# Graph attention on one core: where the head outputs are divided, how one layer's are stored, and at which tiles a head pair's end is issued

## The chip, the cores and the metric

The kernel runs on one core of one Trainium2 chip. The metric is the device time of one execution in microseconds. Engines are named as in the profile: PE is TensorE's matmuls and PEld its weight loads, DVE is VectorE, ACT ScalarE, POOL GpSimd, SP the queue that issues most DMAs. A line such as L598 is a line of the kernel before, unless it is said to be one of the changed kernel.

## The reference

A graph of N = 2708 nodes with 512 features goes through four residual layers, each ended by a layer norm. Layers 0 and 1 are neighbour means with dense weights. Layers 2 and 3 are graph attentions:

```
Wh = h @ W[head]                       8 heads of 64 features
e  = leaky_relu(f1[n] + f2[m], 0.2), masked by the adjacency
head output = softmax(e) @ Wh          heads side by side: [N, 512]
layer 2:  x = layernorm(x + heads)
layer 3:  x1 = elu(heads); one more attention with one head of 512;
          elu, two dense layers; x = layernorm(x + that)
```

A softmax row divides by its sum. The kernel leaves the products with Wh undivided, computes the sums beside them, and divides the outputs.

## The kernel before

The nodes are cut into NT = 22 tiles of 128 rows. The mask lies transposed in SBUF for the whole run (maskT). After layers 0 and 1 the stages that matter here follow each other:

- project (L502, "p2" and "p3") makes Wh of one layer. For each tile, a source function delivers 512 features a row (plain L758 or summed L761), PE transposes them in four 128x128 steps (L120), ACT copies the result to xT (L122), and PE multiplies with the weights in 16 instructions (L529, 32 records a pair of tiles). DVE takes two columns out (dcol L534, b L536) and scales the product into R2 (L543); ACT makes exponentials of the columns (ecol L538, ucol L539, vcol L549, vrow L557). Loads are made one tile ahead, with three buffers for rows. In "p3", summed loads layer 2's head outputs from o_dram and the residual from x2_dram, adds them on DVE (L764), and normalises: bn_stats (L108), bn_aggr (L110), a small addition (L112), a power on POOL (L113), and the multiply on DVE (L114). It stores the row tile through POOL's queue (L766).
- heads_attention (L613, "a2" and "a3") is the long stage. The output nodes are cut into two blocks of 11 tiles (1408 and 1300 wide). For each block and each pair of heads (eight "runs"), a loop goes over 22 tiles j. For each j and head DVE makes the weights e (L598; four buffers, so two tiles j), ACT a comparison c in fp8 (L606; eleven buffers), and PE adds six products to po (L734). Every fourth j, PE adds the divisor products of the last four j to pd from c (L665, "burst").
- The end of a pair is a generator, finish (L668), of which one step is taken in each j of the next pair: the rest of the divisor products and a copy dT (L635); at j=2 the fold of dT into sums by three small matmuls (L643); at j=3, 5 and 7 the turns, transposes of oT in groups of four tiles (L686); behind the first of them the divisor itself by five small DVE operations (rc, L710 to L714); after each turn a DVE multiply that divides and moves the group from PSUM to SBUF (L696) and a store to o_dram (L702, L704). oT is a copy of po that ACT makes at the pair's end (L743).
- masks (L646) makes the part of the sums that needs only the mask, once a block, before the block's first pair is finished: 88 matmuls (L651), for the second block in steps of four j that follow the pair end.
- project "p4" has elu_first (L769) as its source: rows of o_dram, then ELU by four operations (L753 to L756), then the same transposes. last_attention and the dense layers follow. The tile lin (L896) holds their weights and hT; two 2 MB loads (L789, L790) fill it.

The order of TensorE's instructions inside heads_attention is the order in which the code issues them: pe() (L95) chains each to the one before. All other orders are a scheduler's, from program order and its own costs. [...]

Of the kernel before, what the change touches and what calls it, by code (L numbers as in the profile page):

```python
# [30 lines left out]
def kernel(  # L31
# [56 lines left out]
    z1_dram = dram.tile([N, D], F32, name="z1_dram")  # L88
    x2_dram = dram.tile([N, D], F32, name="x2_dram")
    x3_dram = dram.tile([N, D], F32, name="x3_dram")  # L90
    o_dram = [dram.tile([N, D], F32, name=f"o_dram{i}") for i in range(2)]

    behind = []

# [8 lines left out]
    def as_it_comes(ins):  # L103
        return ins

    def layer_norm(pool, y, n, dst):
        st = pool.tile([P, 6], F32, name="ln_st")
        nc.vector.bn_stats(st[:n], y)  # L108
        mv = pool.tile([P, 2], F32, name="ln_mv")
        nc.vector.bn_aggr(mv[:n], st[:n])  # L110
        rs = pool.tile([P, 1], F32, name="ln_rs")
        nc.vector.tensor_scalar(rs[:n], mv[:n, 1:2], EPS, None, op0=OP.add)  # L112
        nc.gpsimd.tensor_tensor(rs[:n], rs[:n], half[:n], OP.pow)  # L113
        nc.vector.tensor_scalar(dst, y, mv[:n, 0:1], rs[:n], op0=OP.subtract, op1=OP.mult)  # L114

    def transposed(pool, psum, src, n, name, order=as_it_comes):

# [368 lines left out]
    ecol = late.tile([P, NT, H], F32, name="ecol")  # L486
    for c in (ucol, ecol, vcol, bcol):
        nc.gpsimd.memset(c, 0.0)
    okc = const.tile([P, 4], F32, name="okc")
    nc.vector.tensor_scalar(rdeg, iso, 0.0, None, op0=OP.is_equal, op1=OP.add, accum_out=okc[:, 3:4])  # L490
    expected = float(P * NT * (3 * H + 1))
# [7 lines left out]
        nc.vector.tensor_sub(rest, rest, dst[:, :, :, 1])  # L499
        nc.vector.tensor_copy(dst[:, :, :, 2], rest)  # L500

    def project(name, source, layer, v_dram, cuts):  # L502


        w_src, w_view, _, heads = atts[layer]
# [9 lines left out]
        with ExitStack() as ph:  # L515
# [4 lines left out]
            width = max(z - a for a, z in cuts) * P  # L520
            xs = early(1, NT, lambda t: source(sm, t, rows(t)))
            xTs = early(0, NT, lambda t: transposed(ahead, ps_tr, xs(t), rows(t), "xT"))
            for t in range(NT):
                n = rows(t)
                xT = xTs(t)
# [84 lines left out]
    cuts = [-((-NT * i) // nb) for i in range(nb + 1)]  # L610
    blocks = list(zip(cuts[:-1], cuts[1:]))

    def heads_attention(name, att, dst):  # L613

        with ExitStack() as ph:
# [28 lines left out]
            def masks(b, p):  # L646

                c00 = att.blocks[b][0] * P
                for j in range(NT):
                    for g, c0, c1 in groups(b):  # L650
                        pe(nc.tensor.matmul(p[32 * g:32 * g + 3 * H, :c1 - c0], parts_m[:, j].rearrange("p h i -> p (h i)"),  # L651
                                            maskT[:, j, c00 + c0:c00 + c1], start=(j == 0), stop=(j == NT - 1)))
                    if j % 4 == 3:
                        yield
                dT = copied(p)
                yield
                ps = folded(dT, pick_m.rearrange("p g h -> p (g h)"))
                yield
                nc.vector.tensor_copy(sums_m[b].rearrange("p (g t) h -> p t g h", g=4), ps)

            def divisors(b, p, pair):
                for j, hs, cs in pair:
# [3 lines left out]
                                                start=(j == 0 and h == hs[0]), stop=(j == NT - 1 and h == hs[1])))  # L666

            def finish(b, h0, p, pair, oT):  # L668
                t0, t1 = att.blocks[b]
                nt = t1 - t0  # L670

                divisors(b, p, pair)
                dT = copied(p)
                yield
                yield
                sums = folded(dT, pick_c.rearrange("p g k q -> p (g k q)")).rearrange("p t g (k q) -> p t g k q", k=2)
                yield
                full = min(t1, FULL) - t0
                rc = sm.tile([P, 12, 2], F32, name="rc")
                by = lambda x_: x_.rearrange("p (g t) k -> p t g k", g=4)  # L680

                def turned(a0):
                    ps = ps_t.tile([P, 512], F32, name="ps_t").rearrange("p (t c) -> p t c", c=P)
                    for t in range(a0, min(a0 + 4, nt)):
                        n = rows(t0 + t)
                        pe(nc.tensor.transpose(ps[:n, t - a0, :], oT[:, a0 // 4, (t - a0) * P:(t - a0) * P + n], ident))  # L686
                    return ps

                def divided(a0, ps):
                    a1 = min(a0 + 4, nt)  # L690
                    o = sm.tile([P, 4, P], F32, name="o", bufs=3)
                    for n, a, z in [(P, a0, min(a1, full)), (rows(NT - 1), max(a0, full), a1)]:
                        if a >= z:
                            continue
                        m = z - a
                        nc.vector.tensor_mul(o[:n, a - a0:z - a0].rearrange("p t (k c) -> p t k c", k=2),  # L696
                                             ps[:n, a - a0:z - a0].rearrange("p t (k c) -> p t k c", k=2),
                                             rc[:n, a:z, :, None].to_broadcast([n, m, 2, HO]))
                        r0 = (t0 + a) * P
                        rows_ = dst[r0:r0 + (m - 1) * P + n, h0 * HO:(h0 + 2) * HO]  # L700
                        if n == P:
                            nc.sync.dma_start(rows_.rearrange("(t p) c -> p t c", p=P), o[:, a - a0:z - a0])  # L702
                        else:
                            nc.sync.dma_start(rows_, o[:n, a - a0])  # L704

                for a0 in range(0, nt, 4):
                    ps = turned(a0)
                    yield
                    if a0 == 0:
                        nc.vector.tensor_mul(by(rc), sums[:, :, :, :, 1], by(vcol[:, t0:t0 + 12, h0:h0 + 2]))  # L710
                        nc.vector.tensor_add(by(rc), by(rc), sums[:, :, :, :, 0])
                        nc.vector.tensor_add(rc, rc, sums_m[b][:, :, h0:h0 + 2])
                        nc.vector.tensor_scalar(rc, rc, 1e-30, None, op0=OP.max)
                        nc.vector.reciprocal(rc, rc)  # L714
                    divided(a0, ps)
                    yield

            sums_m = [sm.tile([P, 12, H], F32, name="sums_m") for b in range(len(att.blocks))]
            for _ in masks(0, pd[1]):
                pass  # L720
            todo = iter(())
            for r, (b, h0) in enumerate(runs):
                w = att.width(b)
                parts = [(c, min(c + 4 * P, w)) for c in range(0, w, 4 * P)]
                hs = (h0, h0 + 1)
                vs = [att.load(b, h) for h in hs]
                po = [ps_o.tile([P, 512], F32, name="po", tag="po") for _ in parts]
                pair = []
                for j in range(NT):
                    es = [att.weights(b, h, j, v) for h, v in zip(hs, vs)]  # L730
                    cs = [att.above(b, h, j, e) for h, e in zip(hs, es)]
                    for i, (c0, c1) in enumerate(parts):
                        for k, (h, e) in enumerate(zip(hs, es)):
                            pe(nc.tensor.matmul(po[i][HO * k:HO * k + HO, :c1 - c0], R2[:, j, h * HO:(h + 1) * HO],  # L734
                                                e[:, c0:c1], start=(j == 0), stop=(j == NT - 1)))
                    if len(pair) == 4:
                        divisors(b, pd[r % 2], pair)
                        pair = []
                    pair.append((j, hs, cs))
                    next(todo, None)  # L740
                oT = sm.tile([P, 3, 512], F32, name="oT", bufs=1)
                for i, (c0, c1) in enumerate(parts):
                    nc.scalar.copy(oT[:, i, :c1 - c0], po[i][:, :c1 - c0])  # L743
                todo = finish(b, h0, pd[r % 2], pair, oT)
                if h0 == H - 4 and b + 1 < len(att.blocks):
                    todo = chain(todo, masks(b + 1, pd[r % 2]))
            for _ in todo:
                pass

    def elu(pool, dst, src, n, w):  # L750

# [8 lines left out]

    def summed(sm, t, n):  # L761

        o, x2 = fetched(o_dram[0], t, n), fetched(x2_dram, t, n, late, "spare", 2)
        nc.vector.tensor_add(o, o, x2)  # L764
        layer_norm(late, o, n, o)
        nc.gpsimd.dma_start(x3_dram[t * P:t * P + n, :], o)  # L766
        return o

    def elu_first(sm, t, n):  # L769
        o = fetched(o_dram[1], t, n)  # L770
        elu(late, o, o, n, D)
        return o

    class Last:
# [111 lines left out]
            pass  # L886

    vd = [dram.tile([heads, N], F32, name=f"v_dram{i}") for i, heads in enumerate((H, H, 1))]
    for i, (source, dst) in enumerate(((plain, o_dram[0]), (summed, o_dram[1]))):
        with ExitStack() as ph:  # L890
            att = Weights(ph, f"a{2 + i}", blocks, vd[i])
            project(f"p{2 + i}", source, i, vd[i], blocks)
            heads_attention(f"a{2 + i}", att, dst)
    ph4 = fast.enter_context(ExitStack())
    att = Weights(ph4, "a4", quads, vd[2])
    lin = ph4.enter_context(tc.tile_pool(name="lin", bufs=1)).tile([P, KD * FF + KF * D + KD * 512], F32, name="lin")  # L896
    project("p4", elu_first, 2, vd[2], quads)


    bad = const.tile([1, 1], mybir.dt.int32, name="bad")  # L900
# [325 lines left out]
```

## Time and profile before

Three runs took 3123.17, 3125.3 and 3129.33 us (median 3125.3); the profiled one has a span of 3125.8 us at a granted clock of 0.996.

| Engine | busy us | share |
|---|---|---|
| PE | 3009.5 | 96% |
| DVE | 1988.8 | 64% |
| ACT | 1401.3 | 45% |
| POOL | 223.2 | 7% |

The shares are an average over stages with different limits, and matmuls are pipelined, so that a busy PE is not PE at its peak; what bounds a stage is read from the waits in it. By the trace the stages stand at: layers 0 and 1 until 925 us, projection 2 until 1025, head attention 2 until 1612, projection 3 until 1715, head attention 3 until 2308, projection 4 until 2404, and the last attention with the dense layers to the end. The copies of oT mark the ends of pairs: 1103, 1178, 1252, 1327, 1396, 1466, 1536 and 1606 us in head attention 2.

### The profile page before, as it was taken

The numbers are of one execution on the slowest core, as the hardware profiler recorded it, in microseconds if no ns is written. First come the engines' busy times: TensorE is split into PE (matmuls) and PEld (weight loads), VectorE is DVE, ScalarE is ACT, GpSimd is POOL, SyncE is SP. The second block draws the span as 40 slices with busy tenths as digits, with TensorE's granted clock in tenths as the row PEclk, the third lists the DMA queues.
The fourth block names the chain that finished last, engine by engine and source line by source line (L and its number), as shares of the span: only waits on it lengthen the run. The fifth ranks groups of instructions, "written<-read, shape, count | busy, mean of one in ns | idle before, by whom it ended". The sixth has DMA issues, their size and how long they took to land.

```text
span 3125.8 us, 37086 instructions
## 1 busy us (share of the span) xinstructions
PE 3009.5 (96%) x14888; PEld 1647.0 (53%) x14888; DVE 1988.8 (64%) x2562; ACT 1401.3 (45%) x1575; POOL 223.2 (7%) x352
## 2 busy tenths in 40 slices
PE   8999999999999999999998999999999999999998
PEld 4556666448887433333356333333356455555555
DVE  5562765212233899999986999999963524345342
ACT  2431000112224688888863788899863000000011
POOL 2220010101110000000012000000000000000001
PEclk9999999999999999999999999999999999999999
DMA  5651421322222000110024010011021000000000
GB/s 137 139 127 35 121 64 41 108 65 81 81 70 76 15 29 35 39 44 30 28 80 145 22 39 28 27 38 33 20 97 48 4 14 17 24 14 22 14 19 21
DMA packets 114287, 163.31 MB, mean 52 GB/s; under 512 B 39494, under 2 KB 62311, under 8 KB 114104
## 3 DMA queue, kind: packets, MB, share of 16 engines
q1 hardware_dynamic: 88152, 109.21, 11.5%
q0 software_dynamic: 16064, 47.95, 5.6%
q10 hardware_dynamic: 9888, 3.67, 0.5%
q8 instruction: 119, 1.95, 0.3%
q14 instruction: 64, 0.52, 0.1%
HBM read 130.92 MB, written 44.55 MB: 56 GB/s over the span
## 4 chain that ended last, share of the span: by engine, by line
PE 65%; issue 19%; DVE 10%; ACT 2%; DMA 2%; POOL 1%; DVEq 0%; POOLq 0%; SPq 0%; ACTq 0%
PE pn L857 13%; PE pm L221 10%; PE po L734 9%; PE acc L450 7%; DVE e L598 6%; PE acc L408 5%; PE pm L529 5%; PE pl L832 5%; PE pl L823 5%; PE pd L665 2%; ACT c L606 1%; PE ps_tr L120 1%; PE acc L254 1%; DMA rows<-o_dram 1%; PE pm L401 1%
## 5 line engine op out<-in xcount | busy, mean ns | idle before, releaser
L598 DVE SCALAR_TENSOR_TENSOR e<-v_bc,ucol,maskT 128x1300 f32<-128x1300 f32 (+3 forms) x836 | 1187.4, 1473 | 345.6 <-PE pn L857 317.9
L606 ACT ACTIVATE c<-e,bcol 128x1300 fp8e4<-128x1300 f32 (+1 forms) x704 | 993.9, 1423 | 113.0 <-DVE e L598 61.7
L734 PE MATMUL po<-e,R 128*64 128x512 f32 (+2 forms) x4224 | 946.4, 550 | 47.4 <-DVE e L598 47.3
L734 PEld LDWEIGHTS po<-e,R 128*64 128x64 f32 x4224 | 340.5, 136 | 600.3 <-issue 384.9
L857 PE MATMUL pn<-e,R 128*128 128x512 f32 (+1 forms) x1056 | 413.5, 542 | 0.0
L857 PEld LDWEIGHTS pn<-e,R 128*128 128x128 f32 x1056 | 191.0, 190 | 199.4 <-issue 195.9
L529 PE MATMUL pm<-w,xT 128*128 128x264 f32 (+3 forms) x1056 | 247.7, 388 | 17.1 <-ACT xT L122 16.6
L529 PEld LDWEIGHTS pm<-w,xT 128*128 128x128 f32 (+1 forms) x1056 | 191.3, 187 | 58.5 <-ACT xT L122 24.4
L408 PE MATMUL acc<-yH,kT 128*128 128x512 f32 x484 | 214.0, 442 | 0.0
L825 ACT ACTIVATE w<-pl,b 128x256 f32<-128x256 f32 (+1 forms) x88 | 40.9, 465 | 372.9 <-PE pl L823 372.9
L450 PE MATMUL acc<-yH,mf 128*128 128x512 f32 x484 | 192.7, 398 | 0.0
L408 PE MATMUL acc<-yL,kT 128*128 128x512 f32 x484 | 192.4, 398 | 0.0
L450 PE MATMUL acc<-yL,mf 128*128 128x512 f32 x484 | 190.2, 393 | 0.0
L221 PE MATMUL pm<-w,xT 128*128 128x512 f32 (+1 forms) x384 | 175.1, 598 | 2.4 <-ACT xT L122 1.4
L113 POOL TENSOR_TENSOR ln_rs<-ln_rs,half 128x1 f32<-128x1 f32 x88 | 51.6, 586 | 1693.0 <-DVE ln_rs L112 1691.7
L221 PE MATMUL pm<-weight,xT 128*128 128x512 f32 (+1 forms) x352 | 162.3, 604 | 3.6 <-DVE weight L133 2.8
L313 DVE SCALAR_TENSOR_TENSOR kT<-pm,maskT 128x512 fp32r<-128x512 f32 (+1 forms) x132 | 84.8, 642 | 123.6 <-PE pm L311 122.9
L832 PE MATMUL pl<-lin,w 128*128 128x512 f32 (+1 forms) x352 | 157.4, 592 | 0.0
L823 PE MATMUL pl<-lin 128*128 128x256 f32 (+1 forms) x704 | 153.4, 371 | 3.7 <-DVE lin L756 3.7
L823 PEld LDWEIGHTS pl<-lin 128*128 128x128 f32 x704 | 129.1, 190 | 34.5 <-issue 15.8
L447 ACT CAST mf<-maskT 128x1024 fp32r<-128x1024 fp8e4 (+1 forms) x66 | 64.3, 976 | 163.2 <-PE acc L450 160.9
L215 ACT CAST yH<-pm 128x512 fp32r<-128x512 f32 (+1 forms) x44 | 25.7, 585 | 245.7 <-PE pm L221 245.7
(172 smaller groups left out, 2518.3 us busy)
## 6 DMA issues: line engine op xcount, KB each, us to landing
rows<-x_dram SPq DMA_DIRECT2D x63, 256.0 KB
m<-in_adj_dram POOLq DMA_DIRECT2D x21, 677.0 KB, 6.3
v_bc<-v_dram SPq DMA_DIRECT2D x16, 704.0 KB
x_dram<-u POOLq DMA_DIRECT2D x42, 256.0 KB, 2.3
rows<-o_dram SPq DMA_DIRECT2D x42, 256.0 KB
v_bc<-v_dram SPq DMA_DIRECT2D x16, 650.0 KB
o_dram<-o SPq DMA_DIRECT2D x32, 256.0 KB
rows<-in_x_dram SPq DMA_DIRECT2D x21, 256.0 KB
```

The source lines that it names most:

```text
L221: order(nc.tensor.matmul(pm[:n], xT[:, k, :n], w[:, k, :], start=(k == 0), stop=(k == KD - 1)))
L313: nc.vector.scalar_tensor_tensor(kT[:, :w], cum[:, :w], KEEP, maskT[:, j, cols], op0=OP.is_le, op1=OP.mult)
L408: nc.tensor.matmul(pa[t], kT[:, (t - b[0]) * P:(t - b[0] + 1) * P], y[:, j, :], start=(j == 0 and y is yH), stop=(j == NT - 1 and y is yL))
L447: nc.scalar.copy(mf[:, :g1 - g0, :], maskT[:, g0:g1, t * P:(t + 1) * P])
L450: nc.tensor.matmul(pa, mf[:, j - g0, :], y[:, j, :], start=(j == 0 and y is yH), stop=(j == NT - 1 and y is yL))
L529: nc.tensor.matmul(pm[a][:n, :D // 2 + heads], xT[:, k, :n], w[:, k, a, :D // 2 + heads], start=(k == 0), stop=(k == KD - 1))
L598: nc.vector.scalar_tensor_tensor(e[:, :w], v[:, :w], ucol[:, j, h:h + 1], maskT[:, j, c0:c0 + w], op0=OP.max, op1=OP.mult)
L606: nc.scalar.activation(c[:, :w], e[:, :w], AF.Sigmoid, bias=bcol[:, j, h:h + 1], scale=STEP, saturate=False)
L734: pe(nc.tensor.matmul(po[i][HO * k:HO * k + HO, :c1 - c0], R2[:, j, h * HO:(h + 1) * HO], e[:, c0:c1], start=(j == 0), stop=(j == NT - 1)))
L823: nc.tensor.matmul(pl[:, :w], self.lin1[:, k, f * P:(f + 1) * P], h[:, k, :w], start=(k == 0), stop=(k == KD - 1))
L832: nc.tensor.matmul(pl[:n], gT[:, f, (t - t0) * P:(t - t0) * P + n], self.lin2[:, f, :], start=(f == 0), stop=(f == KF - 1))
L857: nc.tensor.matmul(pn[k][:, :w], R2[:, j, k * P:(k + 1) * P], e[:, :w], start=(j == 0), stop=(j == NT - 1))
```

## The change

In heads_attention the pair end is no longer a generator but a table of steps by tile j. The rest of the divisor products comes at j=0, the fold at j=4 right after that tile's divisor products, the five small operations at j=6. For layer 2 the first turn comes with the fold at j=4, the other two at j=8, and ACT copies each group to SBUF undivided (at j=5, 9, 10) for the same stores. For layer 3 there are no turns: oT is stored as it is, transposed, to oT_dram. Mask products of the second block come in three lots of eight j at j = 12, 16 and 20. The reciprocals stay in a tile rcs for both blocks and all heads.

The division is done by the next stage. summed multiplies the row tile by rcs before the residual is added, and the layer norm's last step goes to ACT, with one more small DVE operation. In projection 4 elu_turned takes two tiles at a time: it loads the transposed features into the last part of lin (two buffers) and the reciprocals, spread over 64 partitions for each head, from rc_dram through POOL's queue; then a multiply, an exponential and two more operations make xT directly. Reciprocals get to rc_dram by one transpose (spread), a copy and eight stores a block.

```diff
-    o_dram = [dram.tile([N, D], F32, name=f"o_dram{i}") for i in range(2)]
+    o_dram = dram.tile([N, D], F32, name="o_dram")
+    oT_dram = dram.tile([D, N], F32, name="oT_dram")
+    rc_dram = dram.tile([H, NT * P], F32, name="rc_dram")
...
-        nc.vector.tensor_scalar(dst, y, mv[:n, 0:1], rs[:n], op0=OP.subtract, op1=OP.mult)
+        if not on_scalar:
+            nc.vector.tensor_scalar(dst, y, mv[:n, 0:1], rs[:n], op0=OP.subtract, op1=OP.mult)
+            return
+        nc.vector.scalar_tensor_tensor(mv[:n, 0:1], mv[:n, 0:1], -1.0, rs[:n], op0=OP.mult, op1=OP.mult)
+        nc.scalar.activation(dst, y, AF.Identity, bias=mv[:n, 0:1], scale=rs[:n])
...
+            if turned:
+                twos = early(1, -(-NT // 2), lambda i: turned(sm, 2 * i, min(2 * i + 2, NT)))
+                xTs = lambda t: twos(t // 2)[:, :, t % 2 * P:t % 2 * P + P]
...
-                        nc.vector.tensor_mul(o[:n, a - a0:z - a0].rearrange("p t (k c) -> p t k c", k=2),
-                                             ps[:n, a - a0:z - a0].rearrange("p t (k c) -> p t k c", k=2),
-                                             rc[:n, a:z, :, None].to_broadcast([n, m, 2, HO]))
+                        nc.scalar.copy(o[:n, a - a0:z - a0], ps[:n, a - a0:z - a0])
...
+                def spread():
+                    ps = ps_t.tile([P, 512], F32, name="ps_t")
+                    pe(nc.tensor.transpose(ps[:12 * H, :P], rcs[:, b].rearrange("p h t -> p (h t)"), ident))
+                    r = sm.tile([12 * H, P], F32, name="r", bufs=1)
+                    nc.scalar.copy(r, ps[:12 * H, :P])
+                    for h in range(H):
+                        nc.sync.dma_start(rc_dram[h, t0 * P:t1 * P].rearrange("(t p) -> t p", p=P),
+                                          r[12 * h:12 * h + nt])
+
+                steps = {0: [rest], 4: [fold], 6: [divide]}
+                if as_rows:
+                    steps[4].append(lambda: turn(0))
+                    steps[5] = [lambda: store(0)]
+                    steps[8] = [lambda: turn(4), lambda: turn(8)]
+                    steps[9] = [lambda: store(4)]
+                    steps[10] = [lambda: store(8)]
+                else:
+                    nc.sync.dma_start(oT_dram[feats, cols], oT.rearrange("p i c -> p (i c)")[:, :att.width(b)])
+                    if h0 == H - 2:
+                        steps[8] = [spread]
+                return steps
...
-                    next(todo, None)
+                    for step in todo.get(j, ()):
+                        step()
...
-                    todo = chain(todo, masks(b + 1, pd[r % 2]))
+                    products, fold, keep = masks(b + 1, pd[r % 2])
+                    todo.update({12: products[:1], 16: products[1:2], 20: products[2:], NT: [fold], NT + 2: [keep]})
...
+        nc.vector.tensor_mul(by_head, by_head, rcs[:n, b, :, t - blocks[b][0], None].to_broadcast([n, H, HO]))
         nc.vector.tensor_add(o, o, x2)
-        layer_norm(late, o, n, o)
+        layer_norm(late, o, n, o, on_scalar=True)
...
+        o = lin[:, -KD * 512:].rearrange("p (i k n) -> p i k n", i=2, k=KD)[:, t0 // 2 % 2]
+        rc = sm.tile([P, KD, 2 * P], F32, name="rc2")
+        nc.sync.dma_start(o[:, :, :w], oT_dram.rearrange("(k p) n -> p k n", p=P)[:, :, cols])
+        for q in range(2):
+            nc.gpsimd.dma_start(rc[HO * q:HO * q + HO, :, :w],
+                                rc_dram.rearrange("(k q) n -> q k n", q=2)[q, :, cols].partition_broadcast(HO))
+        nc.vector.tensor_mul(o[:, :, :w], o[:, :, :w], rc[:, :, :w])
+        nc.scalar.activation(rc[:, :, :w], o[:, :, :w], AF.Exp)
+        nc.vector.tensor_scalar(rc[:, :, :w], rc[:, :, :w], 1.0, -1.0, op0=OP.min, op1=OP.add)
+        nc.vector.scalar_tensor_tensor(o[:, :, :w], o[:, :, :w], 0.0, rc[:, :, :w], op0=OP.max, op1=OP.add)
```

## The prediction, made before the changed kernel was run

> **What bounds the kernel now.** I read the windows by stage first, then the waits inside the head attentions, then the timelines of VectorE and TensorE there, and last TensorE's timeline in the two projections that follow. Columns of the windows: length, then busy time (instructions) of PE, PEld, DVE, ACT, POOL, clock, DMA share, GB/s. The rows are head attention 2, projection 3, head attention 3 and projection 4.
>
> ```profile
> 1025.00:1612.00 587.00, 560.58 (x3856) 229.38 (x3856) 567.14 (x452) 507.57 (x384) 3.50 (x6) 1.00 0.10 31
> 1612.00:1715.00 103.00, 91.30 (x441) 73.17 (x440) 69.52 (x204) 38.32 (x116) 28.51 (x59) 0.98 0.51 160
> 1715.00:2308.00 593.00, 565.12 (x3870) 230.75 (x3868) 566.75 (x452) 516.80 (x398) 0.42 (x2) 1.00 0.09 29
> 2308.00:2404.00 96.00, 89.74 (x452) 73.44 (x451) 35.74 (x111) 47.08 (x149) 0.00 (x0) 1.00 0.33 107
> ```
>
> In the attentions DVE is busy 97% and PE looks as full, so the waits must decide. Head attention 2's:
>
> ```profile
> PEld po L734 <- DVE e L598: 85.5, 98, 1.7
> PE po L734 <- DVE e L598: 23.0, 58, 0.8
> DVE e L598 <- PE po L734: 9.6, 19, 2.2
> ```
>
> PE waits for the weights e far more than DVE waits for PE: **VectorE's e is the bound there** (12 in 19.31 us is 1.61 us each in the 1408-wide block, 9 in 13.44 us is 1.49 in the 1300-wide one), and PE has bursts that reach it now and then. One such burst, VectorE then TensorE, in the pair that also computes the mask sums:
>
> ```profile
> 1280.76 0.56 DVE L696 TENSOR_TENSOR o<-ps_t,rc 128x384 f32<-128x384 f32 x1
> 1281.23 19.31 DVE L598 SCALAR_TENSOR_TENSOR e<-v_bc,ucol,maskT 128x1408 f32<-128x1408 f32 x12
> 1301.83 6.55 DVE L598 SCALAR_TENSOR_TENSOR e<-v_bc,ucol,maskT 128x1408 f32<-128x1408 f32 x4 [1.28 <-PE po L734]
> ```
> ```profile
> 1294.58 2.58 PE L734 MATMUL po<-e,R 128*64 128x512 f32 x12
> 1297.09 1.15 PE L665 MATMUL pd<-c,parts_c 128*12 128x384 fp8e4 x26
> ...
> 1299.14 2.58 PE L734 MATMUL po<-e,R 128*64 128x512 f32 x12
> 1301.66 0.83 PE L651 MATMUL pd<-maskT,parts_m 128*24 128x384 fp8e4 x16
> ```
>
> Between two po tiles PE spends 2.05 us (1297.09 to 1299.14) on divisor and mask products. e has four buffers, two tiles j of two heads. So DVE can start e of tile j+3 only when PE is through po of j+1: 1294.58 + 2.51 + 2.05 + 2.52 = 1301.66, and 0.17 later, at 1301.83, it goes on after 1.28 us idle. From this **the rule of this prediction**: with B us of other work on PE after po of j, DVE waits 2.52 + B + 2.52 + about 0.22 - 6.42 (four e), that is B - 1.16. A bare divisor burst (B = 1.40) then costs 0.24; the trace has 0.26 at 1226.93 and 1240.05.
>
> In projection 3 two tiles take about 9.6 us, PE's own work being 8.8 (projection 4's steady pace):
>
> ```profile
> 1644.88 4.72 PE L529 MATMUL pm<-w,xT 128*128 128x264 f32 x20 [0.96 <-ACT xT L122]
> 1654.48 4.72 PE L529 MATMUL pm<-w,xT 128*128 128x264 f32 x20 [1.12 <-ACT xT L122]
> ```
>
> The xT copy is late because ACT stands at ecol, which waits for dcol, which stands on DVE behind the layer norm's last multiply, which waits for POOL's pow.
>
> **What the skill says.** "TensorE: Matmul & The Clock Gate", its opening table, calls the queues of ScalarE, VectorE and GpSimd strict FIFO; the chain just named is that, and the trace agrees (DVE idle 0.85 us for ln_rs at 1652.99, the copy behind it). "Perfetto Trace Analysis", section Identifying Performance Opportunities, says that the same gap repeated on the engine that should be saturated can mean too few buffers: the 0.26 us at every divisor burst fits. "ScalarE: Activation LUTs", What ACT_TABLE_LOAD costs, gives an activation with immediates 186 ns + 0.833 ns per column: 0.61 us for 512, where the trace has 0.58 (L743). "DMA: Bandwidth & Descriptors", Anatomy of one DMA, gives, for GpSimd's path, 2.0 us plus bytes over 436 GB/s: 2.6 us for 256 KB, where the page's issues have 2.3.
>
> **Part by part.**
>
> *The divide leaves VectorE.* Per pair of heads three multiplies go (L696: 1.28 and 0.56 us, together about 1.75 net of overlap). The five small operations for rc stay (about 0.5 us). In attention 2 three ScalarE copies of PSUM come instead (0.58, 0.58, 0.48 us); ACT is busy 86% and each c is about 0.2 us shorter than e, 9 us of slack a pair, so they hide. Each copy waits on ACT for its turn, some 1.1 us at j=5, with c of tile 6 queued behind it; e of tile 8, the first to need that c, is 6 us off. In attention 3 copies, transposes and 28 small stores on SP all go; eight stores of 0.7 MB and twice eight of reciprocals take their place, none of which anything in that stage reads.
>
> *The pair end moves beside the divisor products.* Before, fold (0.77 us), turns (0.58, 0.58, 0.47) stand alone behind separate tiles and fit into PE's slack. After, in PE's new order: at j=4 burst + fold + first turn, at j=8 burst + the other two turns; in attention 3 burst + fold at j=4 only. By the rule: attention 2, j=4: B = 1.40 + 0.77 + 0.58 = 2.75, wait 1.6; j=8: B = 2.45, wait 1.3, less 0.3 for rc operations that now fall behind e of j=8, so 1.0. Check on the pair before: 44 x 1.606 = 70.65, + 0.65 (v_bc's DMA) + 0.5 (rc) + 1.75 (divide) + 0.5 (two bursts) = 74.05; the trace has 74.4 and 73.9. After: 70.65 + 0.65 + 0.5 + 2.6 + 0.5 = 74.9, **+0.85**. In the 1300-wide block the same sum gives +1.0. Three and four such ends: +6.5. The very last end overlaps projection 3. Attention 3: B = 2.17, wait 1.0, against 1.75 saved: -0.7, seven times -4.9.
>
> *Mask products of block 1.* Before, six lots of 0.75 us on separate tiles (pair 75.3 us against 74.0: 1.3). After, lots of 32, 32 and 24 at j = 12, 16, 20: B = 2.70, 2.70, 2.4; waits 1.5, 1.5, 1.2 less the 0.26 twice that was there, the third half covered by v_bc's wait, plus 0.4 for the fold at the next pair's rest: 3.4. Net +2.1 in each attention. **Attention 2: +8.6; attention 3: -2.8**, with 0.3 more for the reciprocals' transpose at j=8: -2.5.
>
> *Projection 3.* Its loads and stores are as before. DVE gets a multiply (0.69, as L764) and a small product (0.18) a tile and loses the last multiply (0.55) to ACT (0.6 to 0.8 us). In DVE's new order dcol stands ahead of the small product that waits for POOL, so the head-of-line wait goes: up to 0.8 us of each of some eight free pairs. Against it the chain from a landed row to its transpose gets about 1 us longer, with about 1 us to spare (it ended 1651.5, the transpose came at 1652.8). Bounds -6.5 and +8; I take **-2.5**.
>
> *Projection 4.* Gone: 88 fp32 transposes on PE (0.86 us a tile), so two tiles need 7.15 us (2321.23 to 2328.38) and not 8.78. But the start moves. Before, rows for the first tiles came long before attention 3 ended, and the first product ran at 2305.8. Now the operand lies in lin, in memory that attention 3 used, so its first load waits for the end (2304.0). SP then has eight rc_dram stores (about 0.3 us each) ahead of the second load, and they wait for dT, fold, five rc operations (to 2306.7), a transpose and a copy: 2307.5 + 2.4, load issued 2310.2, landed about 2313.5 (512 KB: 3.2 by the skill's estimate). DVE has the second multiply ahead of the first tile's last two operations: 1.22 + 0.75 + 1.22 (twice the 512 rows' 0.69 and 0.42, less one overhead) + 0.3: first product at about 2317; up to 2320.5 if POOL's rc loads wait for these stores too. From there lin has two buffers: pair i+1's load waits for pair i-1's products, and multiply, exp (1.04), two more operations and semaphores make some 8.5 to 9.7 us after that. Every second pair waits: two pairs take 15.7 to 16.9, not 14.3. End 2317 + 5 x 15.7 + 7.15 = 2402.7, or up to 2410; before 2403.5. I take **+3** (bounds -1 and +7). SP stands at each such load, with the v_dram stores and attention 4's v_bc behind it, which are needed at the end of the stage; 11 loads take the place of 22, and POOL, idle there before, issues 22 of rc. The 11.5 MB in all run where DMA is 33% busy, so I cost them at nothing beyond the chain.
>
> Sum: 8.6 - 2.5 - 2.5 + 3 = **+6.6 on the profiled span of 3125.8**; the three runs' median, 3125.3, stands 0.5 under it, so 3131.9.
>
> **Rivals.** (A) The bursts do not reach VectorE; it keeps all 1.75 us of each of 14 pair ends: -24.5, with projections +0.5: 3101. For it: PE idles 1.4 us of every 13.1. Against: the 1.28 us wait above, at a burst smaller than three of the new ones. It holds if B - 1.16 stays under zero. (B) Projection 4 runs at PE's pace from where it began: 2305.8 + 11 x 7.15 = 2384.5, -19, with the rest +3.6: 3110. It decides on whether the preparation takes less than 7.15 us and the first load less than a3's tail; the SP order speaks against it. (C, clearly slower) The two-buffer chain of projection 4 is longer: if loads of 1 KB rows beside POOL's broadcasts bring it to 11 us, two pairs take 18.2, ending at 2415: +11.4 in place of +3: 3140. It decides from 7.15 us on, and every us over costs 5; projection 3's longer chain at its upper bound gives as much. For C: both chains are in-order and nothing is there to spare; against: DMA was free.
>
> **Numbers.** Forecast 0.45 (own range 3125 to 3139), A 0.20, B 0.10, C 0.25. A measurement here tells 0.2% (6.3 us) from no change. Faster by that, under 3119: A and B, 0.30; slower, over 3131.6: C and half of the forecast, 0.47; the rest 0.23. The range leaves out A and what is past C: 3106 to 3148.
>
> **What would show it.** Right: DVE idle <-PE po of 1.6 us about tile 7 and 1.0 about tile 11 of each pair in attention 2, about 1.0 once in attention 3; three of 1.2 to 1.5 in the mask pair; pairs of 74.9 and 70.6 us in attention 2 and 73.3 and 69 in attention 3; projection 3 at 9 to 9.5 us for two tiles; PE idle some 11 us before projection 4, then pairs alternating 7.2 and 8.5 or more. Wrong: pairs under 73 us in attention 2 (the rule), or a projection 4 under 93 us in all.

## The result, and where the time went

The changed kernel takes 3160.4 us (median of four, 3155.3 to 3167.1) against 3124.6 (3123.2 to 3129.3): a ratio of 1.0113, 95% interval 1.0091 to 1.0135. It is slower by 36 us; the prediction had the sign right and the size, 6.6 us, far off: the time is outside its range. The profiled executions are 3158.8 and 3125.8 us long, 33.0 apart.

The windows by stage again, now of the changed kernel: attention 2, projection 3, attention 3, projection 4. An attention here runs from its first product to the copies of its last pair's output ("the last output copy": where these start), and a projection from there to the next attention's first product.

```profile
1036.40:1617.00 580.60, 549.58 (x3712) 218.22 (x3713) 549.76 (x403) 513.98 (x406) 3.49 (x6) 1.00 0.09 29
1617.00:1741.50 124.50, 108.76 (x599) 83.19 (x595) 80.28 (x252) 61.01 (x152) 30.34 (x61) 0.96 0.48 150
1741.50:2312.20 570.70, 540.57 (x3636) 214.44 (x3637) 543.20 (x385) 504.79 (x380) 0.00 (x0) 1.00 0.07 25
2312.20:2435.60 123.40, 87.14 (x407) 68.70 (x404) 42.66 (x90) 41.25 (x127) 13.60 (x22) 0.88 0.49 135
```

Read the last row first: in projection 4 TensorE is busy 87 of 123 us, and its granted clock is 0.88. The same cuts in both kernels give this table (us):

| | before | after | difference | predicted |
|---|---|---|---|---|
| up to attention 2 | 1033.5 | 1036.4 | +2.9 | 0 |
| attention 2 | 572.3 | 580.6 | +8.3 | +8.6 |
| projection 3 | 122.3 | 124.5 | +2.2 | -2.5 |
| attention 3 | 574.0 | 570.7 | -3.3 | -2.5 |
| projection 4 | 102.6 | 123.4 | **+20.8** | +3 |
| last attention to the end | 721.1 | 723.2 | +2.1 | 0 |

The 2.9 us of the first row are not put down to the change: among the ten kernels below, which leave these stages alone, the same point lies anywhere from 1030.1 to 1034.6. The 2.1 of the last row come after the last store is issued (10.9 us from there to the end before, 13.0 after). Every kernel below that keeps layer 3 transposed has 723.2 to 724.2 here, every one with rows 720.9 to 721.5; no run tells why.

**The attentions** did what the rule said. The waits inside attention 2, changed kernel (who waits, for whom; us in total, times, longest):

```profile
PEld po L772 <- DVE e L612: 107.8, 116, 1.5
PE po L772 <- DVE e L612: 31.0, 84, 0.6
DVE e L612 <- PE po L772: 20.5, 31, 2.1
DVE e L612 <- ACT c L620: 3.1, 2, 1.6
```

VectorE's waits for PE have doubled from 9.6 us to 20.5, and PE's for VectorE have grown as well (85.5 and 23.0 before). VectorE in one pair of the 1408-wide block shows where:

```profile
1202.13 0.19 DVE L707 TENSOR_TENSOR rc<-ps_t,vcol 128x24 f32<-128x24 f32 x1
1202.36 0.20 DVE L709 TENSOR_TENSOR rc<-rc,ps_t 128x24 f32<-128x24 f32 x1
1203.73 1.69 DVE L612 SCALAR_TENSOR_TENSOR e<-v_bc,ucol,maskT 128x1408 f32<-128x1408 f32 x1 [1.18 <-PE po L772]
...
1218.05 12.86 DVE L612 SCALAR_TENSOR_TENSOR e<-v_bc,ucol,maskT 128x1408 f32<-128x1408 f32 x8 [1.18 <-PE po L772]
1231.17 12.85 DVE L612 SCALAR_TENSOR_TENSOR e<-v_bc,ucol,maskT 128x1408 f32<-128x1408 f32 x8 [0.26 <-PE po L772]
```

Two waits of 1.18 us behind the stacked bursts, 0.26 behind a bare one. The first would be 1.57 but for the two operations for rc (0.39) that fill it. Pairs are 74.8 us (predicted 74.9), the pair with the mask sums 79.1.

**Projection 4.** TensorE, then VectorE, at its start:

```profile
2316.98 0.42 PE L736 MATMUL ps_t<-ident,rcs 128*96 128x128 f32 x1 [1.38 <-DVE rcs L712]
2340.24 5.31 PE L543 MATMUL pm<-w,lin 128*128 128x257 f32 x16 [22.84 <-DVE lin L829]
```
```profile
2321.93 0.20 DVE L585 MEMSET sq<- 128x176 f32 x1 [5.09 <-DMA rc_dram<-r]
2332.66 1.23 DVE L826 TENSOR_TENSOR lin<-lin,rc 128x1024 f32<-128x1024 f32 x1 [10.53 <-DMA rc<-rc_dram]
2336.95 1.22 DVE L826 TENSOR_TENSOR lin<-lin,rc 128x1024 f32<-128x1024 f32 x1 [3.06 <-DMA rc<-rc_dram]
```

The first product stands 28.1 us behind the last output copy (3.8 before). Its tile takes 5.31 us where 3.63 is usual: after this gap PE starts at half its clock. The Trainium skill's "TensorE: Matmul & The Clock Gate", section Why this matters for your kernels, warns of PE idle for more than about 3 us; the windows here agree (a granted clock of 0.50 in the 20 us before). VectorE first waits 5.1 us to clear the small tile sq: what ends the wait is the reciprocals' stores, which read r, so sq seems to lie in memory that r used. Then it waits 10.5 us for the reciprocals, whose loads POOL issues at 2322.4, right behind that clearing. What SP issued just ahead of these, and POOL's loads:

```profile
2320.79 0.39 SPq L822 DMA_DIRECT2D lin<-oT_dram  x1
2321.22 0.51 SPq L847 DMA_DIRECT2D lin<-in_L_gnn_lin_w_dram  x1
2321.77 0.50 SPq L848 DMA_DIRECT2D lin<-in_L_gnn_lin_w_dram  x1
2322.42 2.54 POOL L824 DMA_DIRECT2D rc<-rc_dram  x4 [590.23 <-DVE sq L585]
```

SP's last two are loads of 2 MB, the weights of the dense layers (the MLP), which nobody needs before 2529. The windows at that time, and last the one of the kernel before (columns as ahead; the last two are the share of the DMA engines and GB/s):

```profile
2320.00:2330.00 10.00, 0.00 (x0) 0.00 (x0) 0.20 (x1) 0.00 (x0) 2.54 (x4) 0.50 0.83 251
2330.00:2340.00 10.00, 0.00 (x0) 0.00 (x0) 4.24 (x5) 3.40 (x3) 0.00 (x0) 0.50 1.03 298
```
```profile
2310.00:2320.00 10.00, 8.70 (x46) 7.06 (x45) 4.43 (x15) 5.19 (x15) 0.00 (x0) 1.00 1.04 363
```

The kernel before loads the same 4 MB at the same place, at 363 GB/s and a share of 1.04, but its rows for the first tiles had long landed. A small wait of this kind stood in its trace already:

```profile
2315.29 0.16 DVE L536 TENSOR_SCALAR b<-pm 128x1 f32<-128x1 f32 x1 [4.75 <-DMA o_dram<-o]
```

VectorE waited 4.75 us there for the attention's last stores, of which TensorE felt 1.0.

### The profile page after: what moved, and what is told of

Read it like the earlier page. It is cut to its first block, busy times and chain, and to the rows that moved or that the text cites. A ratio compares the mean times of both kernels' runs of the same rounds, so it can differ in the third digit from the quotient of the medians.

```text
span 3158.8 us, 36720 instructions
## 1 busy us (share of the span) xinstructions
PE 2997.2 (95%) x14714; PEld 1630.8 (52%) x14714; DVE 1970.5 (62%) x2495; ACT 1412.4 (45%) x1590; POOL 238.3 (8%) x374
## 4 chain that ended last, share of the span: by engine, by line
PE 65%; issue 17%; DVE 10%; ACT 3%; DMA 3%; POOL 1%; SPq 0%; DVEq 0%; POOLq 0%; ACTq 0%
PE pn L915 13%; PE pm L229 10%; PE po L772 9%; PE acc L458 7%; DVE e L612 6%; PE acc L416 6%; PE pl L890 5%; PE pm L543 5%; PE pl L881 5%; PE pd L685 2%; ACT c L620 2%; PE acc L262 1%; PE ps_tr L128 1%; DMA lin<-oT_dram 1%; PE pm L409 1%
## 5 line engine op out<-in xcount | busy, mean ns | idle before, releaser
L543 PE MATMUL pm<-w,xT 128*128 128x264 f32 (+1 forms) x704 | 170.5, 398 | 9.8 <-ACT xT L130 9.5
L543 PEld LDWEIGHTS pm<-w,xT 128*128 128x128 f32 (+1 forms) x704 | 131.1, 191 | 38.7 <-ACT xT L130 13.5
L881 PEld LDWEIGHTS pl<-lin 128*128 128x128 f32 x704 | 129.2, 190 | 34.4 <-issue 15.8
```

Source lines behind the costliest of these rows:

```text
L543: nc.tensor.matmul(pm[a][:n, :D // 2 + heads], xT[:, k, :n], w[:, k, a, :D // 2 + heads], start=(k == 0), stop=(k == KD - 1))
L881: nc.tensor.matmul(pl[:, :w], self.lin1[:, k, f * P:(f + 1) * P], h[:, k, :w], start=(k == 0), stop=(k == KD - 1))
```

## The experiments

Two questions: do the stacked steps cost what the rule says, and what makes projection 4 long? All kernels are the changed one with an edit. Times are medians; ratios are to the kernel before on the same chip (3126.4 to 3127.2 there). The stages are cut as in the table, from one profiled execution of each kernel.

**Steps apart.** No step stands beside divisor products any more:

```diff
-                steps = {0: [rest], 4: [fold], 6: [divide]}
+                steps = {0: [rest], 2: [fold], 6: [divide]}
                 if as_rows:
-                    steps[4].append(lambda: turn(0))
-                    steps[5] = [lambda: store(0)]
-                    steps[8] = [lambda: turn(4), lambda: turn(8)]
-                    steps[9] = [lambda: store(4)]
-                    steps[10] = [lambda: store(8)]
+                    steps[3] = [lambda: turn(0)]
+                    steps[4] = [lambda: store(0)]
+                    steps[5] = [lambda: turn(4)]
+                    steps[6].append(lambda: store(4))
+                    steps[7] = [lambda: turn(8)]
+                    steps[9] = [lambda: store(8)]
...
-                    todo.update({12: products[:1], 16: products[1:2], 20: products[2:], NT: [fold], NT + 2: [keep]})
+                    todo.update(dict(zip((10, 11, 13, 14, 15, 17), ([q] for q in products))))
+                    todo.update({19: [fold], 21: [keep]})
```

(six lots of four j in place of three of eight; spread at j=9)

> The changed kernel, with the steps of a pair's end on tiles that have no divisor products after them (fold at j=2, the three turns at 3, 5 and 7, their copies one or two tiles later), and block 1's mask products in six lots on such tiles too. Burst theory (VectorE pays what PE does between two po tiles, beyond 1.16 us): its idle time behind po in the two attentions falls from 36 us to under 12, pairs of the 1408-wide block in attention 2 from 74.8 to 72.3, in attention 3 from 73.6 to 72.5; attention 2 is 564 to 567 us long in place of 580.6, attention 3 about 562 in place of 570.7; in all 3132 to 3138. Rival (what a pair's end costs is the work itself, the copies on ScalarE and the small operations, wherever it stands): pairs stay at 74 to 75 us, in all 3156 to 3162.

Measured: 3136.6 us, ratio 1.0028 (1.0019 to 1.0036). Attention 2 is 563.4 us long, attention 3 564.0; pairs are 72.9 (expected 72.3 and 72.5), the mask pair 73.7. The wait of attention 2 that had doubled:

```profile
DVE e L612 <- PE po L773: 10.7, 30, 2.1
```

It is near its old value, with the divide gone from VectorE as well. The burst theory stands, and the rival falls. Two details were off. The waits for PE of both attentions fell from 36.0 to 20.9 us, not to under 12: a bare burst still costs 0.26 us in the 1408-wide block and 0.35 in the other, which the expectation left out. Attention 3 came out 2 us longer than expected, most of it in one pair of 70.0 among those of 68.3.

**Rows in projection 4.** Attention 3 stores rows as attention 2 does, and projection 4's source is

```diff
-            heads_attention(f"a{2 + i}", att, i == 0)
+            heads_attention(f"a{2 + i}", att, True)
...
-    project("p4", None, 2, vd[2], quads, elu_turned)
+    project("p4", elu_first, 2, vd[2], quads)
...
+    def elu_first(sm, t, n):
+        o = fetched(o_dram, t, n)
+        b = next(i for i, (a, z) in enumerate(blocks) if a <= t < z)
+        by_head = o.rearrange("p (h c) -> p h c", h=H)
+        nc.vector.tensor_mul(by_head, by_head, rcs[:n, b, :, t - blocks[b][0], None].to_broadcast([n, H, HO]))
+        elu(late, o, o, n, D)
+        return o
```

> The changed kernel, with layer 3 kept as rows as layer 2 is: attention 3 turns and stores rows, projection 4 reads them, divides them on VectorE, applies the ELU and transposes on PE. Operand theory (projection 4's 21 us come from the way its transposed operand arrives: memory that is free only when attention 3 ends, one chain of stores and loads, two buffers): from attention 3's last output copy to the last attention's first product 103 to 107 us in place of 123.4, attention 3 as long as attention 2 (580 in place of 570.7); in all about 3152 (3148 to 3156). Rival (the stage is long because PE's clock has fallen, or because of what the attention leaves behind): the stage stays over 115 us, in all 3162 or more.

Measured: 3150.1 us, ratio 1.0069 (1.0052 to 1.0086). Projection 4 is 102.7 us, its first product 3.8 after the last copy, exactly as in the kernel before, although the divide is now in it; attention 3 is 584.1 (expected 580). So the 20.8 us come from the transposed form of layer 3, its storing and loading, and neither from the divide nor from a lower clock that the stage would have had anyway.

**Weights held.** Two VectorE copies of one element each, made with the operand of tiles 12 and 13, write into the weights' memory, so their loads must wait:

```diff
         nc.vector.scalar_tensor_tensor(o[:, :, :w], o[:, :, :w], 0.0, rc[:, :, :w], op0=OP.max, op1=OP.add)
+        if t0 == 12:
+            for m in (0, KD * FF):
+                nc.vector.tensor_copy(lin[0:1, m:m + 1], o[0:1, 0, 0:1])
         return o
```

> The changed kernel, with the two 2 MB loads of the MLP's weights held back until tiles 12 and 13's operand is made (one element of each target is written by VectorE then); nothing else is moved. Contention theory (the first rc loads land 8 us late because 4 MB went out ahead of them): rc lands by 2327 in place of 2332.5, projection 4's first product comes 5 to 7 us earlier after attention 3's end than 28.1 us; in all 3153 to 3156. Rival (the chain of stores, waits and loads itself is that long): the first product within 1.5 us of before, in all 3159 to 3161.

Measured: 3158.9 us, ratio 1.0098 (1.0081 to 1.0114): the time is at the rival's figure, but the start is as the theory has it. The first multiply:

```profile
2322.28 1.23 DVE L826 TENSOR_TENSOR lin<-lin,rc 128x1024 f32<-128x1024 f32 x1 [5.58 <-DMA rc<-rc_dram]
```

VectorE waits 5.6 us for the reciprocals in place of 10.5. The multiply starts 15.4 us after the last copy (20.5 in the changed kernel) and the first product 21.2 (28.1), 6.9 earlier; the two runs with other edits that leave the start of this stage alone have 27.9 and 28.6. Then the rest of the stage takes 103.0 us. A window at the place where the weights went:

```profile
2390.00:2400.00 10.00, 8.28 (x40) 6.66 (x38) 1.46 (x5) 2.45 (x10) 1.18 (x2) 1.00 1.05 284
```

The DMA engines are full again (1.05), the next pair's load is late, PE waits 4.2 us at 2402, and the 16 products after that take 6.40 us. What the weights cost at this place is less sure than at the start: the rest of the stage is 95.4 us in the changed kernel, but 99.9 and 100.5 in those two other runs.

**Four buffers.** Operand and reciprocals each get four buffers in the weights' memory, which holds the weights back to the end of the stage. So this run changes three things at once: the number of buffers, where the reciprocals lie, and when the weights are loaded.

```diff
-        o = lin[:, -KD * 512:].rearrange("p (i k n) -> p i k n", i=2, k=KD)[:, t0 // 2 % 2]
-        rc = sm.tile([P, KD, 2 * P], F32, name="rc2")
+        o = lin[:, -2 * KD * 512:].rearrange("p (i k n) -> p i k n", i=4, k=KD)[:, t0 // 2 % 4]
+        rc = lin[:, :2 * KD * 512].rearrange("p (i k n) -> p i k n", i=4, k=KD)[:, t0 // 2 % 4]
...
-                twos = early(1, -(-NT // 2), lambda i: turned(sm, 2 * i, min(2 * i + 2, NT)))
+                twos = early(2, -(-NT // 2), lambda i: turned(sm, 2 * i, min(2 * i + 2, NT)))
```

> The changed kernel, with four operand buffers and four rc buffers, all in the memory of the MLP's weights (which are then loaded at the stage's end), and operands made two pairs ahead. Two-buffer theory: pairs of tiles come at 7.2 us in place of 8.5, and rc, no longer in memory that attention 3's last step uses, is loaded some 8 us earlier: first product 10 to 16 us after attention 3's last output copy in place of 28.1; the stage 92 to 99 us in place of 123.4; in all 3131 to 3137. Rival (pace set by the loads themselves or by the order on VectorE's and POOL's queues): pairs stay at 8 to 8.5 us and the stage at 105 to 112; in all 3143 to 3150.

Measured: 3150.0 us, ratio 1.0063 (1.0046 to 1.0079), in the rival's range. The stage is 114.1 us, nearer the rival's figure: first product at 19.9 (expected 10 to 16), the rest 94.2. VectorE shows why the start gained less:

```profile
2324.95 0.69 DVE L828 TENSOR_SCALAR lin<-lin 128x1024 f32<-128x1024 f32 x1 [1.12 <-ACT lin L827]
2329.56 0.20 DVE L585 MEMSET sq<- 128x176 f32 x1 [3.91 <-DMA rc_dram<-r]
2329.68 1.16 DVE L829 SCALAR_TENSOR_TENSOR lin<-lin 128x1024 f32<-128x1024 f32 x1
```

POOL's loads now go out 2.6 us after the last copy (10.2 in the changed kernel). The reciprocals are there, three of four operations are done, and the fourth stands behind the clearing of sq. As for the pace, the last 16 tiles come at 3.8 us each, 7.6 a pair; the same tiles take 8.6 a pair in the changed kernel. So the two buffers, filled one pair ahead, do cost about 1 us a pair. The first pairs lose it again: eight broadcasts of reciprocals start at once, and the loads of the second to fourth operand are issued only behind the eight stores, from 2324.7.

**sq apart.** The same, with sq in a buffer that attention 3 doesn't use:

```diff
-            sq = sm.tile([P, NT, H], F32, name="sq", bufs=1)
+            sq = (late.tile([P, D], F32, name="spare", bufs=2)[:, :NT * H].rearrange("p (t h) -> p t h", h=H) if turned else
+                  sm.tile([P, NT, H], F32, name="sq", bufs=1))
```

> The run with four operand buffers, and the small tile sq of projection 4 in memory that attention 3 does not use, so that VectorE's clearing of it waits for nothing. Theory (that clearing stood on VectorE until the reciprocals' eight stores had landed, with the first pair's last operation behind it): first product 14 to 17 us after attention 3's last output copy in place of 19.9; in all 3144 to 3147. Rival (the stores and loads crowd each other whatever VectorE does): 19 us or more, in all 3149 to 3151.

Measured: 3147.1 us, ratio 1.0061 (1.0046 to 1.0076). The first product comes at 16.1, 3.8 earlier: the clearing did hold it. The stage as a whole, 113.9, gained nothing, and the two ratios are alike. VectorE:

```profile
2332.81 1.23 DVE L827 TENSOR_TENSOR lin<-lin 128x1024 f32<-128x1024 f32 x1 [2.94 <-DMA lin<-oT_dram]
...
2338.76 0.15 DVE L550 TENSOR_SCALAR b<-pm 128x1 f32<-128x1 f32 x1
```

That b is of tile 0, whose products ran long before. It stands behind the operands of the next three pairs, and these wait for their loads; TensorE, which transposes b, waits 7.4 us for it. Work made further ahead can so put the oldest tile's small operation behind the newest tile's load in the same queue.

**Projection 3's layer norm on VectorE.**

```diff
-        layer_norm(late, o, n, o, on_scalar=True)
+        layer_norm(late, o, n, o)
```

> The changed kernel, with the layer norm of projection 3 applied by VectorE's one instruction again (the multiply by rcs stays). Theory that the move to ScalarE is what lengthened projection 3 (a second hop VectorE to ScalarE to PE, with ScalarE's own queue in front): from attention 2's last output copy to attention 3's first product 121.5 to 123 us in place of 124.5; in all about 3158. Rival (the added multiply by rcs lengthens the chain, and the move to ScalarE relieves VectorE as I had thought): 125.5 to 129; in all 3161 to 3165.

Measured: 3151.9 us, ratio 1.0077 (1.0062 to 1.0092), under both ranges. Projection 3 is 119.3 us, 5.2 under the changed kernel and 3.0 under the one before, with the multiply by rcs still in: a larger gain than the theory had. The changed kernel there, for one pair of tiles, VectorE, ScalarE and TensorE (other rows left out):

```profile
1665.05 0.16 DVE L121 SCALAR_TENSOR_TENSOR ln_mv<-ln_mv,ln_rs 128x1 f32<-128x1 f32 x1 [0.47 <-POOL ln_rs L117]
...
1665.25 0.81 ACT L122 ACTIVATE rows<-rows,ln_mv,ln_rs 128x512 f32<-128x512 f32 x1 [3.08 <-DVE ln_mv L121]
...
1665.97 0.19 ACT L563 ACTIVATE vcol<-b 128x8 f32<-128x8 f32 x1
...
1666.57 0.21 ACT L552 ACTIVATE ecol<-dcol 128x8 f32<-128x8 f32 x1 [0.41 <-DVE dcol L548]
...
1666.78 0.56 ACT L130 COPY xT<-ps_tr 128x512 f32<-128x512 f32 x1
...
1667.40 3.83 PE L543 MATMUL pm<-w,xT 128*128 128x264 f32 x16 [0.63 <-ACT xT L130]
```

The layer norm's last step (L122) waits on ScalarE for VectorE's small product, which waits for POOL. It stands in ScalarE's queue ahead of vcol, ecol and the copy xT, on which TensorE waits. So the wait for POOL was not removed: VectorE's part of it is 6.5 us in this stage (8.4 before), and ScalarE now stands in the same chain.

**The edits together.** Rows and steps apart; the same with the layer norm on VectorE; the transposed form with steps apart, four buffers, sq apart and the norm on VectorE; and that last one with the first two tiles' operand in the buffers of rows and of their transposes, which no attention uses:

```diff
+    def turned_tile(t):
+        cols = slice(t * P, t * P + P)
+        o = ahead.tile([P, KD, P], F32, name="xT")
+        rc = ahead.tile([P, D], F32, name="rows", bufs=3).rearrange("p (k n) -> p k n", k=KD)
+        nc.sync.dma_start(o, oT_dram.rearrange("(k p) n -> p k n", p=P)[:, :, cols])
+...
     def elu_turned(sm, t0, t1):
+        if t0 == 0:
+            return [turned_tile(t) for t in range(t0, t1)]
...
```

> The changed kernel with both edits of before: the steps of a pair's end on separate tiles, and layer 3 kept as rows and divided in projection 4. If the burst and operand theories hold and their effects add: attention 2 563 to 564 us, attention 3 564 to 568, projection 4 103 to 104; in all 3107 to 3114, faster than both kernels (the kernel before has 3127 on this chip). Rival (ScalarE's copies of rows and SP's 28 stores in attention 3 collide with the steps spread out): attention 3 574 or more, in all 3118 to 3125.

> The run with rows in layer 3 and steps apart, and projection 3's layer norm applied by VectorE's one instruction. If the move to ScalarE lengthened projection 3: 121.5 to 123 us there, in all 2 us under the run without this edit (3105 to 3112). Rival (the move relieves VectorE): 125.5 to 129, in all 1 to 5 us over it.

> Layer 3 kept transposed as in the changed kernel, with every edit that helped: steps apart, four buffers, sq apart, projection 3's layer norm on VectorE. If the effects add: attention 2 and 3 563 to 565 us, projection 4's stage 112 to 115 with its first product at 15 to 17; in all 3116 to 3123, above the run with rows (3112.7). Rival (the stores and turns of rows cost as much as projection 4 gains): 3112 or less.

> The run before, with the first two tiles' operand in memory that no attention uses (the buffers of rows and of their transposes), so that it is loaded and worked on during attention 3. Theory (what projection 4 loses at its start is that nothing of the operand can be there before attention 3 ends): first product 3 to 5 us after the last output copy, the second pair's 12 to 14; stage 92 to 100 us, at the price of 3 us of VectorE in attention 3; in all 3100 to 3112. Rival (the second pair stands in the same chain as the first did, so the gap only moves behind the first two tiles): second pair's products at 16 us or later, stage 104 or more, in all 3112 to 3120.

| | us | ratio to before (95%) | att. 2 | proj. 3 | att. 3 | proj. 4 | first product |
|---|---|---|---|---|---|---|---|
| rows, steps apart | 3115.1 | 0.9963 (0.9949 to 0.9977) | 563.2 | 126.2 | 565.7 | 102.7 | 3.1 |
| and norm on VectorE | 3112.7 | 0.9950 (0.9937 to 0.9964) | 563.3 | 124.9 | 566.2 | 102.3 | 3.1 |
| transposed, all edits | 3119.9 | 0.9976 (0.9969 to 0.9983) | 563.0 | 121.8 | 563.3 | 112.4 | 15.4 |
| and first pair ahead | 3106.1 | 0.9937 (0.9924 to 0.9951) | 562.7 | 122.2 | 563.9 | 99.7 | 1.9 |

All four beat both kernels, and the last is the fastest found: 21 us under the kernel before, 54 under the changed one. Its interval still overlaps that of the second row. The first came out a us above what was expected, with projection 3 at 126.2 us (123.7 to 125.7 in the other runs with the norm on ScalarE). The norm on VectorE gave only 1.2 us there, not the 5.2 of the run by itself, and 124.9 lies in neither range: over all runs projection 3 is 119.3 to 124.9 (mean 122.1 of four) with it on VectorE and 123.7 to 126.2 (mean 124.8 of seven) on ScalarE. 2.7 is the better figure, with one trace for each run and two ranges that touch.

Of the last run's 21 us, 20 are in the two attentions (1126.6 us in place of 1146.4), and the two rows above with layer 3 kept as rows have 17 of them. So the gain stands where the divide left VectorE, once no step of a pair's end stands beside divisor products, and it is most of the 24.5 us that rival A had forecast. The transposed form by itself was slower than rows (3119.9 against 3112.7) until the first pair had memory of its own.

In the last run, TensorE:

```profile
2286.01 4.93 PE L545 MATMUL pm<-w,xT 128*128 128x257 f32 x22
2296.71 1.20 PE L545 MATMUL pm<-w,lin 128*128 128x257 f32 x2 [5.76 <-issue]
```

The first two tiles follow the attention at once; the second pair is 15.8 us behind the last copy (2280.9; expected 12 to 14), nearly the rival's 16, and 5.8 us of gap remain; the stage, at 99.7, and the time are in the theory's ranges. Attention 3 did not get the 3 us longer that VectorE's work for two tiles would cost.

## Why the prediction was wrong

**Attention 2, +8.6 (measured +8.3), and attention 3, -2.5 (-3.3): right** in the mechanism, and near in size. The waits stood where the rule put them, 1.18 and 1.18 us (predicted 1.6, of which rc's 0.39 are filled, and 1.0), the pairs at 74.8 and 73.6 (74.9 and 73.3), the narrow ones at 70.0 to 71.0 and 68.8 to 69.2 (70.6 and 69); and the run with steps apart took 17 and 7 us away. Rival A does not hold for this kernel. Two things were less good than the sums. In attention 2 two errors cancelled: the mask pair stood out from its neighbours by 4.3 us where it had stood out by 1.2, +3.1 and not +2.1, and the narrow pairs grew by 0.3 to 1.3 us, 3.1 in all and not 4.0. And the rule does not fit the example that it was drawn from: B = 2.05 gives 0.89, the trace 1.28. Nor did every divisor burst cost 0.26: in the kernel before two of a pair's did.

**Projection 4, +3 (+20.8): the step that failed**, by 18 of the 26 us that the sum missed. The first product was put at 2317, 14.9 us after the last copy; it came 28.1 after it. Of these 13 us:

- About 7 are the MLP's weights. I wrote that "the 11.5 MB in all run where DMA is 33% busy, so I cost them at nothing beyond the chain". The 33% was the stage's mean; in the ten microseconds that mattered the trace of before showed the engines full. With the weights held the first product comes at 21.2.
- The rest is the reciprocals' memory and queue. I gave POOL's wait for the stores 3.5 us as an upper bound and took the lower; it happened, by way of the clearing of sq, which I did not list at all: it waits for the stores, and POOL's loads are issued only after it. With four buffers, where these loads no longer wait, the first product is at 19.9, and with sq apart at 16.1. ScalarE's switch of table to exp (1.28 us, between the first multiply and its exponential) was not in the chain either.

The rest of the stage was 95.4 us against the 90.7 that +3 leaves for it: a pair took 8.43 us, at the upper end of the 7.85 to 8.45 that the two-buffer chain gave (8.8 and 8.9 in the two runs that leave the stage alone), and for tiles at half clock there was no term. The operand's load, priced at 3.2 us by a fit for GpSimd's path although SP issues it, took 3.9 where it can be read (issued at 2349.2, waited for until 2353.0). Rival C had the right stage and direction, but it put the price on the pace, where the larger loss was the start.

**Projection 3, -2.5 (+2.2): the sign failed.** The step "so the head-of-line wait goes" did not hold. VectorE still waits for POOL 12 times in this stage, 6.5 us (14 times and 8.4 before), and the added ScalarE instruction, which waits for the same chain, stands in the queue that makes the transposes' copies. Two tiles took 10.0 us in the lines above and around them (1667.40 to 1677.40), not 9 to 9.5. With the instruction back on VectorE the stage is as long as before, 122.1 us in the mean. The bound of +8 covered it.

The remaining 5 us that the sum missed lie before attention 2 and after projection 4, where it had nothing; their cause stays open.

The misses are of one kind: each operation was priced on its own engine, and what queues behind it on the next (ScalarE's copies, VectorE behind the clearing of sq, the reciprocals behind 4 MB) was taken as free.

## What to carry to other kernels

Steps that each fit into an engine's slack cost little apart and much together (attention 2 is 563.4 us with them apart, 580.6 with them stacked): stack them only up to the slack between two buffers' releases, here an estimated 1.16 us. Before an operand is moved into memory that the stage before still holds, list what the first load, its store, the clearing of neighbours and every large load in front of it in the queues will wait for; a few buffers outside that memory for the first tiles were worth 13 us here. Read the DMA share at the moment of need, not the stage's mean.

## What the runs showed of the hardware

A gap on TensorE costs more than its length. After 22.8 us idle, the next 16 products took 5.31 us in place of 3.63, and in the run with the weights held, after 16.1, 6.61. Shorter gaps do it too: in projection 2 of the changed kernel, idle times of 0.99 and 2.49 us with 0.9 us of work between them were followed by 16 products in 6.38 us, not 3.83, and the granted clock is 0.50 from 988.4 to 995.2. How often it happens varies from run to run. With the same code in projection 4, the clock fell to 0.50 again after the start for 3.4 us in the changed kernel, where the stage took 123.4 us; for 13.7 us, in three stretches, in the run that only moved projection 3's layer norm (128.4 us); and for 10.2 us in the run with steps apart (128.4 us).

The reciprocals' eight stores of 5.5 KB landed slowly beside loads. In the run with four buffers they began at 2316.8 with eight broadcasts in flight and let sq go only at 2329.6, at a DMA share of 1.03; in the changed kernel, without the broadcasts, they began at 2317.7 and let it go at 2321.9, at a share of 0.25.
